# Moving the last layer's patch work and weight rounding from layer 2's attention into layer 1's expert loop

## The chip, the cores and the metric

The kernel runs on one core of a Trainium2 chip. It is one program with one launch. The metric is the device time of one execution in microseconds (us). The time before is 2178.75 us, the median of three runs (2176.64 to 2182.37). Engines are named as in the profile: PE (TensorE matmul), PEld (its weight loads), DVE (VectorE), ACT (ScalarE), POOL (GpSimd), SP (SyncE, which here only issues transfers). A "q" after a name is that engine's queue of instructions.

## The reference

The input x has 32 sequences of 128 tokens with 128 features. Four layers follow, each with an attention-like block over a context of 32 x 128 x 256 and a feed-forward block, both added to x behind a tanh gate:

```python
x = x + tanh(g_xattn[0]) * L0_xattn(ctx, layernorm(x), ...)   # 16 heads, masked by length
x = x + tanh(g_ffn[0])   * L0_ffn(layernorm(x), ...)          # gated MLP, hidden 512
x = x + tanh(g_xattn[1]) * L1_xattn(layernorm(x), ctx, ...)   # 16 heads over context and self
x = x + tanh(g_ffn[1])   * L1_ffn(layernorm(x), ...)          # causal attention, then 8 experts, top 2
x = x + tanh(g_xattn[2]) * L2_xattn(ctx, layernorm(x), ...)   # 8 heads, masked
x = x + tanh(g_ffn[2])   * L2_ffn(layernorm(x), ...)          # 8 experts, top 2
x = x + tanh(g_xattn[3]) * L3_xattn(layernorm(x), ctx, lens)  # patches, below
x = x + tanh(g_ffn[3])   * L3_ffn(layernorm(x), ...)          # ternary weights, 8-bit activations
```

What matters here are two parts of layer 3 that depend on no earlier layer. The first is the patch side of its attention-like block. It reads only the context and the patch lengths:

```python
h_patch = rmsnorm(ctx, g_init)[..., :128]
bidx = cumsum(lens, axis=1) - 1                   # where patches end
boundary = zeros.at[arange(B)[:, None], bidx].set(1)
s = scan(s[t] = a * s[t-1] + u[t])                # a decaying sum over 128 patches
plug = clip(cumsum(boundary, axis=1) - 1, 0, 127)
depool = s[arange(B)[:, None], plug]              # added to layernorm(x)'s projection later
```

The second is the rounding of three 512 x 128 weight matrices to -1, 0 and 1 by the mean of their absolute values.

## The kernel before

The 32 sequences are handled in 8 groups of NB = 4; x stays in SBUF for the whole kernel. The stages, in order, are:

- layer 0 and layer 1 (attention, MLP, causal attention), until about 1260 us of the profiled execution;
- layer 1's experts (`routes1.run`, called at L1214);
- layer 2's attention, from about 1420 us (`attend` at L1371), with the routing of its tokens to experts;
- layer 2's experts (`routes2.run`, L1391) from about 1782 us;
- layer 3, from about 1980 us, which reads `depool`, `wq` and `winv`.

**Layer 1's experts.** Tokens lie in DRAM in blocks of 512, sorted by expert. `Routes.run` is a generator that handles 23 such tiles: 8 with a fixed expert, 15 whose expert is read from a table that is made on the way (`tables`). For each tile, `load` issues the expert's weights `w` (three buffers) and the tokens `xt` on SP's queue. `first` turns the tokens (four PE transposes, `tpe` L838), copies them to `xT` on ACT (L1196), and makes the hidden values: PE `p` (L1203, L1205), ACT `sil` (L1207), DVE `hid` (L1208). `second` multiplies by the second weight (PE `ye` L851) and evicts on ACT (`yT` L1212); `third` turns the result back (four PE transposes), copies it on DVE (`yt` L858) and stores it through SP (L859). The generator yields once after the first two loads, once after the table, and once for each tile, 25 times in all. The caller's loop does nothing with these yields:

```python
for _ in routes1.run(pool, psum, e1_d, E1, turned, swiglu, 2, finish):
    pass
```

In the same stretch POOL clears the eight buffers that layer 2's attention will use for its stacked queries and keys (`Slots`, two memsets each, L355 and L357). These are written in the program ahead of the experts.

**Layer 2's attention.** A `Pipe` runs the attention in turns. Each group has two units of four heads, and each unit two turns. A turn computes scores `sc` (PE L561) and their maxima `mx` (DVE L592), then for an earlier turn the transposed scores `sct` (PE), weights `w` (ACT L627) and products `av` (PE L644). Beside the turns go `before(g)` (adds the experts' results, normalises, makes queries), `after(g)` (adds the attention output, normalises, routes the tokens), the indirect transfers of tokens on POOL (`got` L886, `by_expert_r` L699), and a list called `fill`: generators that are advanced by one piece, that is to their next `yield`, twice a turn (`beside`).

**The last layer's generator.** `last_layer()` (L1236) is the only entry in layer 2's `fill` (L1323). Its pieces are:

1. once: the lengths are cast (`lens` L1240), summed by a matmul (`pe` L1242), and made into end positions (L1244 to L1247);
2. for each of the 8 groups, six pieces: (a) a 0/1 matrix of the ends (`hot` L1253) and two loads from the context on SP (`ck` L1257, `cv` L1259); (b) four small matmuls (`cnt` L1263), their minimum (`bound` L1266), and the root mean square of `ck` and `cv` (`rms_scale`: eight `bst` L218, `bmv`, `ms` and the addition of epsilon L207 on DVE, then the power `r` L208 on POOL); (c) the scaling of `ck` (four, L1271); (d) the decaying sum as one matmul (`pd` L1276), evicted on ACT (`dep` L1278); (e) the running count of ends (`pg`, four, L1284) and the one-hot matrix that selects patches (`pick` L1289, L1290); (f) the bias (L183) and the selection (`pdp`, four, L1295), evicted on ACT (L1299) and stored by SP (`depool` L1300);
3. once: the sums of the three weight matrices (`sums` L1306, `pm` L1310, `wsc`, `winv`);
4. three times: one weight matrix is rounded (`wt` L1318, L1319, `wq` L1320).

That is 1 + 8 x 6 + 1 + 3 = 53 pieces. `ck`, `cv`, `hot`, `dep` and `pick` have one buffer each, so a group's load waits until the group before it has finished with the buffer.

A matmul in float takes two passes, so one matmul in the source is two MATMUL records.

**What sets the order.** The framework puts the instructions of each engine into one in-order queue. The queue is not simply the order of the text: an instruction that waits for data may be passed by a later one that does not. Earlier text goes first where both could run. The sums of the weights (L1306), written last, run at 1420.05 us, before anything else of the generator but the lengths.

Of the kernel before, what the change touches and what calls it, by code (L numbers as in the profile page):

```python
# [12 lines left out]
F32 = mybir.dt.float32  # L13
F32R = mybir.dt.float32r
BF = mybir.dt.bfloat16
I32 = mybir.dt.int32
AF = mybir.ActivationFunctionType
ALU = mybir.AluOpType
AX = mybir.AxisListType
PSUM = bass.MemoryType.PSUM  # L20
DRAM = bass.MemoryType.DRAM

P = 128
# [49 lines left out]
def tile_flamingo_gated(  # L73
# [149 lines left out]
    def bc(a, n=D):  # L223
        return a[:, :, None].to_broadcast([a.shape[0], a.shape[1], n])

    def rms_scale(pool, *parts):

        mv = moments(pool, *parts)
        ms = pool.tile([P, NB], F32, tag="st", name="ms")
        nc.vector.tensor_tensor(ms, mv[:, :, 0], mv[:, :, 0], ALU.mult)  # L230
        nc.vector.tensor_tensor(ms, ms, mv[:, :, 1], ALU.add)
        return rsqrt(pool, ms)
# [52 lines left out]
    def flat(a):  # L285
        return a.rearrange("p b s -> p (b s)")
# [900 lines left out]

    with ExitStack() as outer:
        slots2 = outer.enter_context(tc.tile_pool(name="slots2", bufs=1))
        queries = Slots(slots2, "q2", 4, 8, (64, 96), (nc.gpsimd,))  # L1190
        keys = Slots(slots2, "k2", 4, 8, engines=(nc.gpsimd,))
        with ExitStack() as stack:
            pool, psum = mlp_pools(stack, "f1")

            def turned(xT, tp):
                nc.scalar.mul(xT, tp, COL(col, "g2"))  # L1196

            def swiglu(w, xT):
                hid = pool.tile([P, 2, 512], F32, tag="hid", name="hid", bufs=3)
                for f in range(2):  # L1200
                    fs = slice(f * P, (f + 1) * P)
                    p1 = psum.tile([P, 512], F32, tag="h", name="p1", bufs=3)
                    nc.tensor.matmul(p1, lhsT=E1(w, "w1")[:, fs], rhs=xT, start=True, stop=True)  # L1203
                    p3 = psum.tile([P, 512], F32, tag="h", name="p3", bufs=3)
                    nc.tensor.matmul(p3, lhsT=E1(w, "w3")[:, fs], rhs=xT, start=True, stop=True)  # L1205
                    sil = pool.tile([P, 512], F32, tag="sil", name="sil", bufs=3)
                    nc.scalar.activation(sil, p1, AF.Silu)  # L1207
                    nc.vector.tensor_tensor(hid[:, f, :], p3, sil, ALU.mult)  # L1208
                return hid

            def finish(yT, w, y):
                nc.scalar.copy(yT, y)  # L1212

            for _ in routes1.run(pool, psum, e1_d, E1, turned, swiglu, 2, finish):  # L1214
                pass


        with ExitStack() as stack:
# [14 lines left out]
            stacks = Stacks(8, 16, queries, [keys], "bias2")  # L1233
            at2, gots = {}, {}

            def last_layer():  # L1236


                lens = pool.tile([P, B], F32, tag="lens", name="lens", bufs=1)
                nc.vector.tensor_copy(lens, lens_i)  # L1240
                pe = psum.tile([P, B], F32, tag="tp", name="pe")
                nc.tensor.matmul(pe, lhsT=CST(cst, "tri"), rhs=lens, start=True, stop=True)  # L1242
                ends = pool.tile([P, B], F32, tag="ends", name="ends", bufs=1)
                nc.vector.tensor_scalar(ends, pe, -1.0, None, ALU.add)  # L1244
                wrap = pool.tile([P, B], F32, tag="wrap", name="wrap", bufs=1)
                nc.vector.tensor_scalar(wrap, ends, 0.0, float(P), ALU.is_lt, ALU.mult)
                nc.vector.tensor_tensor(ends, ends, wrap, ALU.add)  # L1247
                bound = pool.tile([P, B], BF, tag="bound", name="bound", bufs=1)
                yield
                for g in range(NG):  # L1250
                    bs = slice(g * NB, (g + 1) * NB)
                    hot = pool.tile([P, NB, P], BF, tag="hot", name="hot", bufs=1)
                    nc.vector.tensor_tensor(  # L1253
                        hot, CST(cst, "iota_s")[:, None, :].to_broadcast([P, NB, P]), bc(ends[:, bs], P), ALU.is_equal,
                    )
                    ck = pool.tile([P, NB, D], F32, tag="ck", name="ck", bufs=1)
                    nc.sync.dma_start(out=ck, in_=ctx_all[bs, :, 0:D].rearrange("b s d -> s b d"))  # L1257
                    cv = pool.tile([P, NB, D], F32, tag="cv", name="cv", bufs=1)
                    nc.sync.dma_start(out=cv, in_=ctx_all[bs, :, D:].rearrange("b s d -> s b d"))  # L1259
                    yield  # L1260
                    cnt = psum.tile([P, NB], F32, tag="tp", name="cnt")
                    for b in range(NB):
                        nc.tensor.matmul(  # L1263
                            cnt[:, b : b + 1], lhsT=hot[:, b, :], rhs=ones_b[:, 0:1], start=True, stop=True
                        )
                    nc.vector.tensor_scalar(bound[:, bs], cnt, 1.0, None, ALU.min)  # L1266

                    r = rms_scale(pool, ck, cv)
                    yield
                    for b in range(NB):  # L1270
                        nc.vector.scalar_tensor_tensor(  # L1271
                            ck[:, b, :], ck[:, b, :], r[:, b : b + 1], ROW(row, "g_init"), ALU.mult, ALU.mult
                        )
                    yield
                    pd = psum.tile([P, NB, D], F32, tag="tp", name="pd")
                    nc.tensor.matmul(flat(pd), lhsT=CST(cst, "decay"), rhs=flat(ck), start=True, stop=True)  # L1276
                    dep = pool.tile([P, NB, D], F32, tag="dep", name="dep", bufs=1)
                    nc.scalar.copy(dep, pd)  # L1278
                    yield

                    pg = psum.tile([P, NB, P], F32, tag="tp", name="pg")
                    for b in range(NB):
                        at = g * NB + b
                        nc.tensor.matmul(  # L1284
                            pg[:, b, :], lhsT=bound[:, at : at + 1].to_broadcast([P, P]), rhs=CBF(cbf, "tri"),
                            start=True, stop=True,
                        )
                    pick = pool.tile([P, NB, P], F32, tag="pick", name="pick", bufs=1)
                    nc.vector.tensor_scalar(flat(pick), flat(pg), -1.0, 0.0, ALU.add, ALU.max)  # L1289
                    nc.vector.tensor_scalar(flat(pick), flat(pick), float(P - 1), iota_p, ALU.min, ALU.is_equal)  # L1290
                    yield
                    po = psum.tile([P, NB, D], F32, tag="tp", name="pdp")
                    with_bias(po, "b_in")
                    for b in range(NB):
                        nc.tensor.matmul(  # L1295
                            po[:, b, :], lhsT=pick[:, b, :], rhs=dep[:, b, :], start=False, stop=b == NB - 1,
                            skip_group_check=True,
                        )
                    nc.scalar.copy(dep, po)  # L1299
                    nc.sync.dma_start(out=depool[g], in_=flat(dep))  # L1300
                    yield

                names = ("gate", "up", "down")
                sums = pool.tile([P, 3], F32, tag="sums", name="sums", bufs=1)
                for i, n in enumerate(names):
                    nc.vector.tensor_reduce(  # L1306
                        sums[:, i : i + 1], W3(w3, n), AX.X, ALU.add, apply_absolute_value=True
                    )
                pm = psum.tile([P, 3], F32, tag="tp", name="pm")
                nc.tensor.matmul(pm, lhsT=ones, rhs=sums, start=True, stop=True)  # L1310
                wsc = pool.tile([P, 3], F32, tag="wsc", name="wsc", bufs=1)
                nc.vector.tensor_scalar(wsc, pm, 1.0 / (D * 512), 1e-5, ALU.mult, ALU.max)
                nc.vector.reciprocal(wsc, wsc)
                nc.vector.reciprocal(winv, wsc)
                yield
                for i, n in enumerate(names):
                    t = pool.tile([P, 512], F32, tag="pick", name="wt", bufs=1)
                    nc.vector.tensor_scalar(t, W3(w3, n), wsc[:, i : i + 1], MAGIC, ALU.mult, ALU.add)  # L1318
                    nc.vector.tensor_scalar(t, t, -MAGIC, -1.0, ALU.add, ALU.max)  # L1319
                    nc.vector.tensor_scalar(wq[n], t, 1.0, None, ALU.min)  # L1320
                    yield

            pipe.fill.append(last_layer())  # L1323

            def before(g):
                if g == 0:
# [302 lines left out]
```

## Time and profile before

| | |
|---|---|
| three runs, median (lowest to highest) | 2178.75 us (2176.64 to 2182.37) |
| the profiled execution's own time | 2170.34 us |
| its span | 2168.5 us |
| mean granted PE clock | 0.86 |
| PE busy | 1658.0 us, 76% of the span |
| DVE busy | 1197.4 us, 55% |
| ACT busy | 894.0 us, 41% |
| POOL busy | 638.6 us, 29% |
| sixteen memsets on POOL | 1261.27 to 1317.40 us |
| first pieces of the generator | 1419.9 us (lengths), 1440.2 us (first matmul) |
| last piece | ends at about 1688.4 us |

The profile has one execution. Its page gives each engine's busy time, the span in 40 slices, the chain of waits that ended last, and the costliest groups of instructions. The trace behind it answers narrower questions: busy times and the granted clock in chosen stretches (the table by stage), the instructions in order of time, one line's or one tile's instructions, and who waited for whom. Times are counted from the start of the span. A line with "x4" merges four instructions; the number ahead of the engine is the time from the first one's start to the last one's end. What stands in brackets with an arrow is the idle time before the line and what ended it. Matmuls overlap, so a single one's duration is longer than its step to the next.

### The profile page before, as it was taken

How to read it: one execution, taken by the hardware profiler on the slowest of the kernel's cores; microseconds unless marked ns; L12 is line 12 of the kernel's file. 1: busy time of each engine (PE TensorE's matmuls, PEld its weight loads, DVE VectorE, ACT ScalarE, POOL GpSimd, SP SyncE). 2: the span in 40 equal slices, each digit the busy share in tenths (PEclk: the TensorE clock that was granted, in tenths of full speed). 3: DMA queues.
4: the chain of work that ended last, by engine and by line, in shares of the span. 5: the costliest groups of instructions: out<-in, count | busy, mean ns of one | idle time of the engine just before them, and what ended most of it. 6: DMA issues, size and time to landing. Idle time of an engine off the chain costs nothing.

```text
span 2168.5 us, 35498 instructions
## 1 busy us (share of the span) xinstructions
PE 1658.0 (76%) x13624; PEld 1010.3 (47%) x13624; DVE 1197.4 (55%) x3504; ACT 894.0 (41%) x1110; POOL 638.6 (29%) x637
## 2 busy tenths in 40 slices
PE   0599998989999999878777569926666629995355
PEld 0455445456656666555455424414555514442223
DVE  7645446475545476766666433357667631113797
ACT  0376565565787745333323223301111204441244
POOL 5101101020000012454544482056443430003550
PEclk9999999999999999987877779966667759997566
DMA  6564558634332343112212035435344212332110
GB/s 214 154 230 154 187 184 266 219 101 124 105 100 67 94 145 84 51 54 59 56 48 55 25 116 174 141 104 148 110 124 121 71 63 101 135 132 86 41 49 20
DMA packets 164536, 244.66 MB, mean 113 GB/s; under 512 B 20560, under 2 KB 102288, under 8 KB 164112
## 3 DMA queue, kind: packets, MB, share of 16 engines
q1 hardware_dynamic: 156176, 225.62, 34.0%
q0 software_dynamic: 8192, 16.79, 2.7%
q8 instruction: 107, 1.75, 0.4%
q14 instruction: 61, 0.50, 0.1%
HBM read 139.74 MB, written 101.24 MB: 111 GB/s over the span
## 4 chain that ended last, share of the span: by engine, by line
PE 40%; DVE 14%; POOL 13%; issue 8%; ACT 2%; DMA 2%; SPq 0%; POOLq 0%; DVEq 0%; ACTq 0%
PE ye L851 5%; PE ph L1382 4%; PE av L644 4%; POOL by_expert_r L699 4%; PE sct L561 4%; POOL got L886 3%; PE sc L561 3%; PE ph L1037 3%; PE p L1203 2%; PE tpe L838 2%; DVE mx L592 2%; PE p L1205 2%; PE tp L282 1%; POOL r L208 1%; POOL w L249 1%
## 5 line engine op out<-in xcount | busy, mean ns | idle before, releaser
L627 ACT ACTIVATE w<-sct 128x1024 f32<-128x1024 f32 x288 | 292.8, 1024 | 346.4 <-PE sct L561 345.2
L592 DVE TENSOR_REDUCE mx<-sc 128x8 f32<-128x1024 f32 x160 | 194.9, 1220 | 130.0 <-PE sc L561 129.6
L561 PEld LDWEIGHTS <-stack_q 96*128 96x128 bf16 x2560 | 194.4, 110 | 134.5 <-issue 104.3
L886 POOL DMA_INDIRECT got<-by_expert_r,slot_r x128 | 127.7, 998 | 360.8 <-issue 335.0
L597 DVE TENSOR_REDUCE mx<-sc 128x4 f32<-128x1024 f32 x128 | 152.9, 1222 | 132.8 <-PE sc L561 132.3
L644 PE MATMUL av<-w,va 128*9 128x128 f32 (+2 forms) x3584 | 198.1, 295 | 36.7 <-POOL w L630 31.9
L561 PE MATMUL sc<-stack_k,stack_q 96*128 96x128 bf16 x1536 | 145.7, 244 | 46.8 <-DMA stack_k<-k 17.4
L561 PE MATMUL sct<-stack_q,stack_k 128*128 128x128 bf16 (+1 forms) x1536 | 139.5, 236 | 17.3 <-DVE mx L592 8.3
L561 PEld LDWEIGHTS <-stack_k 128*128 128x128 bf16 (+1 forms) x1536 | 111.8, 107 | 69.6 <-issue 66.6
L644 PEld LDWEIGHTS av<-w,va 128*9 128x9 f32 (+2 forms) x3584 | 98.6, 94 | 87.5 <-POOL w L630 43.5
L851 PE MATMUL ye<-hid,w 128*128 128x512 f32 x276 | 133.4, 593 | 2.3 <-DVE hid L1208 2.3
L311 POOL CAST hml<-whole 128x512 bf16<-128x512 f32 (+1 forms) x48 | 30.1, 626 | 343.0 <-ACT whole L310 166.7
L1037 PE MATMUL ph<-h,w 128*128 128x512 f32 x256 | 123.7, 610 | 1.8 <-ACT hn L1040 0.9
L1037 PE MATMUL ph<-hn,w 128*128 128x512 f32 x256 | 121.2, 604 | 0.7 <-ACT hn L1040 0.7
L208 POOL TENSOR_TENSOR r<-r,m 128x4 f32<-128x4 f32 x56 | 58.5, 1044 | 188.8 <-DVE r L207 175.0
L561 PE MATMUL sc<-stack_l,stack_q 96*128 96x128 bf16 x1024 | 110.4, 238 | 0.0
L650 ACT COPY ot<-av 128x512 f32<-128x512 f32 x112 | 65.5, 584 | 99.5 <-PE av L644 96.6
L630 POOL TENSOR_SCALAR_AFFINE_SELECT w<-w 128x1024 f32<-128x1024 f32 x64 | 70.8, 1106 | 113.9 <-ACT w L627 113.7
L561 PE MATMUL sct<-stack_q,stack_l 128*128 128x128 bf16 x1024 | 98.9, 234 | 2.7 <-DVE mx L592 2.7
L627 ACT ACT_TABLE_LOAD x72 | 92.4, 1283 | 9.7 <-PE sct L561 8.5
L699 POOL DMA_INDIRECT by_expert_r<-yn,slot_r x64 | 65.6, 1025 | 83.1 <-DVE slot_r L757 25.4
L656 PE MATMUL tpo<-cst,ot 128*128 128x128 f32 x448 | 82.4, 306 | 9.5 <-ACT ot L650 6.9
(295 smaller groups left out, 3290.5 us busy)
## 6 DMA issues: line engine op xcount, KB each, us to landing
by_expert_r<-zeros SPq DMA_DIRECT2D x40, 1024.0 KB
stack_q<-q SPq DMA_DIRECT2D x96, 288.0 KB
stack_k<-k SPq DMA_DIRECT2D x96, 288.0 KB
k<-hml SPq DMA_DIRECT2D x16, 1152.0 KB
w<-in_e_dram SPq DMA_DIRECT2D x23, 514.5 KB
xt<-by_expert_r SPq DMA_DIRECT2D x46, 256.0 KB
by_expert_r<-yt SPq DMA_DIRECT2D x46, 256.0 KB
q<-hml SPq DMA_DIRECT2D x72, 128.0 KB
```

Source lines behind the costliest of these rows:

```text
L208: nc.gpsimd.tensor_tensor(r, r, m05.to_broadcast([P, NB]), ALU.pow)
L561: nc.tensor.matmul(dst[:, h * P : (h + 1) * P], lhsT=stat[rows, 4 * e + h, b], rhs=mov[rows, 4 * e + h, b], start=start and h == e == 0, s ...
L592: latest["maxima"] = nc.vector.tensor_reduce(mx[:, :, b0 : b0 + 2].rearrange("p h b -> p b h"), sc.rearrange("p i (h k) -> p i h k", h=4), ...
L597: nc.vector.tensor_reduce(mx[:, :, b0], sc.rearrange("p i (h k) -> p h i k", h=4), AX.XY, ALU.max, negate=True,)
L627: latest["weights"] = nc.scalar.activation(w.rearrange("p i h k -> p i (h k)"), sc, AF.Exp)
L644: nc.tensor.matmul(av[32 * h : 32 * h + dv + 1, b * P : (b + 1) * P], lhsT=values[c][:, b, 4 * u + h, :], rhs=w[:, i, h, :], start=c == 0, ...
L656: nc.tensor.transpose(tp[:, b].rearrange("p s r -> p (s r)"), ot[:, b, :], ident)
L699: ins = nc.gpsimd.indirect_dma_start(out=self.rows(), out_offset=bass.IndirectOffsetOnAxis(ap=slots, axis=0), in_=rows, in_offset=None,)
L851: nc.tensor.matmul(y, lhsT=w2[:, f, :], rhs=hid[:, f, :], start=f == 0, stop=f == n_f - 1)
L886: ins = nc.gpsimd.indirect_dma_start(out=got[:, k, b, :], out_offset=None, in_=self.rows(), in_offset=bass.IndirectOffsetOnAxis(ap=self.sl ...
L1037: nc.tensor.matmul(ph, lhsT=wt[:, c, f * P : (f + 1) * P], rhs=h[:, c, :], start=c == 0, stop=c == 3)
L1382: nc.tensor.matmul(ph, lhsT=E2(w, "w1")[:, f * P : (f + 1) * P], rhs=xT, start=True, stop=True)
```

## The change

The generator is moved ahead of layer 1's experts, unchanged but for its pools. Its SBUF tiles come from a pool of their own, `patches`, which lives through layer 1's experts and layer 2. Its PSUM tiles come from `place[0]`: in the expert loop one bank of a new pool, in layer 2 the three shared banks that it used before. The caller of the expert loop now advances the generator twelve times at the first yield and once at each of the others; layer 2's `fill` gets what is left of it.

```diff
     with ExitStack() as outer:
         slots2 = outer.enter_context(tc.tile_pool(name="slots2", bufs=1))
+        patch_pool = outer.enter_context(tc.tile_pool(name="patches", bufs=2))
+        place = [None]
+
+        def last_layer():
+            lens = patch_pool.tile([P, B], F32, tag="lens", name="lens", bufs=1)
+            nc.vector.tensor_copy(lens, lens_i)
+            pe = place[0].tile([P, B], F32, tag="tp", name="pe")
...
+            yield
+            for g in range(NG):
...
+                ck = patch_pool.tile([P, NB, D], F32, tag="ck", name="ck", bufs=1)
+                nc.sync.dma_start(out=ck, in_=ctx_all[bs, :, 0:D].rearrange("b s d -> s b d"))
...
+        patches = last_layer()
         queries = Slots(slots2, "q2", 4, 8, (64, 96), (nc.gpsimd,))
...
-            for _ in routes1.run(pool, psum, e1_d, E1, turned, swiglu, 2, finish):
-                pass
+            place[0] = stack.enter_context(tc.tile_pool(name="patches_ps", bufs=1, space=PSUM))
+            for i, _ in enumerate(routes1.run(pool, psum, e1_d, E1, turned, swiglu, 2, finish)):
+                for _ in range(12 if i == 0 else 1):
+                    next(patches)
...
-            def last_layer():
-                lens = pool.tile([P, B], F32, tag="lens", name="lens", bufs=1)
...
-            pipe.fill.append(last_layer())
+            place[0] = psum
+            pipe.fill.append(patches)
```

## The prediction

> **What bounds the kernel now.** I read the table by stage first, with stretches cut at the borders of layer 1's experts (1265 to 1414 us, 23 tiles) and of layer 2's attention (1440 to 1745), because the change takes work from the second and puts it into the first.
>
> ```profile
> core 0: us, PE busy (x) PEld busy (x) DVE busy (x) ACT busy (x) POOL busy (x), PEclk, DMA share, GB/s
> 1265.00:1288.00 23.00, 20.02 (x57) 9.48 (x57) 11.84 (x20) 8.31 (x13) 22.83 (x7) 0.87 0.29 100
> 1288.00:1351.00 63.00, 62.11 (x199) 29.50 (x199) 19.80 (x30) 23.14 (x40) 29.17 (x9) 1.00 0.58 176
> 1351.00:1414.00 63.00, 63.00 (x200) 29.59 (x198) 19.80 (x30) 24.06 (x41) 0.00 (x0) 1.00 0.43 136
> 1560.00:1620.00 60.00, 35.77 (x340) 27.85 (x338) 40.48 (x168) 9.75 (x14) 34.17 (x35) 0.68 0.44 127
> 1620.00:1690.00 70.00, 47.41 (x478) 39.78 (x478) 49.61 (x215) 14.31 (x20) 27.36 (x28) 0.72 0.40 115
> 1690.00:1745.00 55.00, 37.59 (x456) 31.14 (x455) 32.94 (x138) 13.73 (x18) 18.87 (x18) 0.74 0.21 62
> ```
>
> Columns are start and end, then busy time by engine. PE is the bound of the experts: busy 63.00 of 63 us at clock 1.00, while DVE has 31% and ACT 38%. In layer 2 nothing is: PE is 60 to 68% busy at clock 0.68 to 0.74, DVE 60 to 71%, POOL 34 to 57%; the stage is a chain through in-order queues. So a piece moved into the experts is free on DVE and ACT, and is paid in full on PE.
>
> The order of time at the start of the experts shows a second thing:
>
> ```profile
> 1268.29 6.98 POOL L357 MEMSET stack_q<- 32x4096 bf16 x2
> 1272.08 3.23 DVE L801 CAST table<-row 1x30 int32<-1x30 f32 x1
> 1272.17 3.14 DVE L1208 TENSOR_TENSOR hid<-p,sil 128x512 f32<-128x512 f32 x2
> 1275.33 6.97 POOL L355 MEMSET stack_q<- 128x4096 bf16 x2
> 1275.39 1.13 PE L851 MATMUL ye<-hid,w 128*128 128x512 f32 x2 [2.28 <-DVE hid L1208]
> ...
> 1310.44 6.96 POOL L357 MEMSET stack_k<- 3x4096 bf16 x2
> ```
>
> Sixteen memsets of 3.51 us fill POOL from 1261.27 to 1317.40. A DVE cast of 30 numbers lasts until the memset beside it ends (3.23 us), hid behind it too, and PE idles 2.28 us.
>
> **The change, part by part.** The generator has 53 pieces: 1 for the lengths, 6 for each of 8 groups, 1 for the sums, 3 for the weights. The expert loop yields 25 times (loads, table, 23 tiles), so 12 + 24 = 36 pieces move: the lengths, groups 0 to 4 whole, and five of group 5. The other 17 stay at the head of layer 2's fill.
>
> *PE in the experts.* Prices at clock 1.00 come from steps between matmuls of one line:
>
> ```profile
> 1412.34 1.88 PE L851 MATMUL ye<-hid,w 128*128 128x512 f32 x4
> ...
> 532.39 0.89 PE L1099 MATMUL po<-wa,oT 128*128 128x128 f32 x6
> ...
> 531.22 0.40 PE L561 MATMUL sct<-stack_q,stack_k 128*128 128x128 bf16 x4
> ```
>
> A float pass of 512 columns steps by (1.88 - 0.59)/3 = 0.43, of 128 columns by (0.89 - 0.275)/5 = 0.12 (0.107 to the next line's start), a bf16 one by 0.056. Per group: pd L1276 2 x 0.43 = 0.86; pdp L1295 8 x 0.11 = 0.88; its bias L183, 512 columns of bf16, 0.22; pg L1284 4 x 0.056 = 0.22; cnt L1263 4 x 0.06 = 0.25. That is 2.43 us. Five groups 12.2, group 5 without pdp and bias 1.3, pe L1242 0.1: **+13.6 us**, all on the path, as PE has no free time there. Below: a tile's period is 6.26 us (p L1203 starts at 1288.34, 1294.60, 1300.86) and its own steps add to 12 x 0.43 + 8 x 0.107 = 6.0, so 0.25 a tile is open; with a piece in two gaps of three, some 4 us of the 13.6 would be hidden. I take none, as PE already waits there for xT on ACT, whose queue gets longer.
>
> *Queues in the experts.* DVE gets about 6.4 us a group (hot 0.68, 8 statistics at 0.2, 4 ck at 0.35, pick 0.69 + 0.48, some 1.5 in small ones), beside 43 us of free DVE in every 63; ACT gets 11 dep copies of 0.59, beside 39 free. Cover gone, a dep copy ahead of xT L1196 costs up to 0.59. SP gets 12 context loads (0.4 to 0.57 each) and 5 depool stores (0.35), between weight loads that already wait there for ye (53.2 us in all): a ck load stuck behind one comes up to a tile late, and bst, then hid, wait on DVE. A depool store that waits for its dep copy on ACT holds the weight, token and result transfers behind it on SP; a pd that waits for ck on DVE holds the next tile's p and ye behind it on PE. POOL gets 6 powers r of 1.04, all emitted behind the memsets: group 0's r cannot start before 1317.4, tile 8, so the pieces behind it bunch up and are worked off from there. For these mismatches, some 25 PE pieces at 0 to 0.3 us: between 0 and 8, I take **+3**.
>
> *The start.* Three DVE instructions of the cast's kind come under the memsets: lens L1240, wrap L1246, and the 128x4 addition in group 0's r (L207). The first has nothing behind it but its own chain; each other can hold DVE up to one memset, 3.5 us, before hid of tile 0, which ends PE's wait. Bounds 0 and 7; I take one, **+3.5**. Sum in the experts: **+20**, between 10 and 29.
>
> *Layer 2.* What goes is read twice. The chain of waits holds the pieces often; one group's passage:
>
> ```profile
> 1580.67 1.05 POOL r L208
> 1581.73 0.03 issue
> 1581.75 1.58 DVE ck L1271 x4
> 1583.34 0.04 issue
> 1583.38 2.07 PE pd L1276 x2
> ```
>
> PE stood for r and ck and then ran pd. Adding all chain rows of such pieces from 1503 to 1666 (r, ck, hot, pick, bst, pd, pdp) gives 27 us. That is the upper end: another wait stands behind each. The other reading compares like with like, cutting at the ends of the 16 output copies ot L650, one for half a group:
>
> ```profile
> 1645.20:1664.38 19.18, 11.77 (x118) 10.39 (x117) 11.98 (x43) 2.76 (x5) 8.76 (x9) 0.64 0.56 161
> 1664.38:1682.24 17.86, 12.03 (x120) 9.70 (x119) 13.79 (x60) 3.80 (x5) 4.11 (x5) 0.81 0.29 89
> 1682.24:1700.31 18.07, 14.35 (x117) 11.72 (x117) 11.53 (x50) 2.86 (x4) 6.02 (x5) 0.55 0.36 106
> ```
>
> None of these has a fetch (got L886 ends at 1609). With the half before (17.91), full fill costs 18.55 a half; with about half the fill (pdp of group 7, the weights) 17.97. So a whole fill is worth 2 x 0.58 = 1.2 us a half, and 36 pieces, four a half, are 9 halves: 10.5 us. Prologue work is no part of it: POOL's fetches bind 1420 to 1500, and the 17 remaining pieces lie there as the first 13 do now. I take **-13**, nearer the like-for-like row, since it contains what takes the chain's place.
>
> Of the clock the rows say that it stood at 0.68 where PE was 60% busy, at 0.72 and 0.74 where it was 68%, at 1.00 where it was full. A rule of the Trainium skill speaks against the change here: "TensorE: Matmul & The Clock Gate", Part 1, says that the clock is throttled unless PE's recent activity releases it. By that rule the thinner layer 2 would run its remaining matmuls slower: a fall of 0.03, my estimate, on some 60 us that PE holds of that chain is 2.5 us, and the sum would be +9.5 instead of +7. My sum goes without it.
>
> **Sum.** 13.6 + 3 + 3.5 - 13 = +7 us. The profiled execution took 2170.34 (span 2168.5), 8.4 below the median of 2178.75; on the median it gives **2186**. A measurement can tell about 0.3% of this kernel, 6.5 us, from no change.
>
> **The rivals.**
> 1. *The chain's rows count in full: faster.* Layer 2 gives 27 us and the experts cost only 10 to 17: -10 to -17, about 2165. The place is the PE queue of layer 2, where scores wait behind pd and pdp. It decides from 20 us on, 2.2 us a half. For it: the passage above, 5.5 us in one group. Against: halves with less fill are hardly shorter.
> 2. *The start hurts twice.* Both stalls (7), mismatches of 8, PE 13.6, give 29; with layer 2 at -10, +19 to +22: 2198 to 2201.
> 3. *Group 0's r blocks a queue.* If DVE's or PE's queue has ck or pd of group 0 ahead of a tile's work, it stands until 1317: some 45 us more, about 2225. Against: the queue orders follow lengths of work, not the text; stack_k's loads, written in layer 2, go out at 1294.74 on SP, shortly after that slot's memset, and SP waited for no memset in that stage.
> 4. *Nothing net.* The gaps hide 4 us and the start costs nothing: 13.6 - 13, about 2179.
>
> **How the numbers follow.** Forecast 40% (own range 2181 to 2192; 13 of it within 0.3%, 27 above), rival 1 30% (faster), rival 2 15%, rival 3 5%, rival 4 10% (7 within, 3 faster). Faster 0.33, same 0.20, slower 0.47. The range of 2160 to 2208 goes from rival 1's lower end (2162) with 2 us more to the experts' upper 29 with nothing won back; outside stay rival 3 and the tails of 1 and 2.
>
> **What would show it.** The 23 tiles should end about 20 us later against their start, PE still full, and more so from tile 8 on, where pieces bunch; hid of tile 0 should start later than 1275.3, measured from the first memset. No r of these groups before the sixteenth memset's end. Layer 2 from its first fetch to its last store should be shorter by 13, with pd's 16 passes at 592 ns and not 1061. I am wrong if the halves fall to 16 us or less (rival 1), or if PE idles for tens of us before 1317 (rival 3).

## The result, and the profile after

The changed kernel took 2193.88 us (median of 5 runs, 2190.1 to 2194.67), the kernel before 2178.75 (5 runs, 2176.37 to 2182.37): 1.0065 times the time, 95% interval 1.005 to 1.008. It is slower, by some 15 us (0.65%) where I had 7. The profiled execution of the changed kernel took 2190.1 us (span 2188.1), 3.8 below its median.

This number can't be understood without one thing that the experiments brought out: layer 2's attention runs in two ways, with the same instructions, a *quick* one and a *slow* one. The changed kernel's runs above are slow ones, and the one profile of before that the forecast was read from was quick.

By stage, cut at the first expert's weight load (L827), the first fetch of layer 2 (L886) and the first weight load of layer 2's experts:

| stage, us | before, profile | changed, profile | difference | predicted |
|---|---|---|---|---|
| up to the experts | 1261.0 | 1255.8 | -5.2 | 0 |
| layer 1's experts | 159.8 | 181.1 | +21.3 | +20 |
| layer 2's attention | 360.5 | 364.1 | +3.6 | -13 |
| the rest | 387.1 | 387.1 | 0 | 0 |

Up to the experts every engine has the same instructions in the same order in both, so the -5.2 is not the change's. The experts by stage, changed kernel (start and end, length, busy time of PE, its weight loads, DVE, ACT and POOL with instruction counts, granted clock, DMA share, GB/s):

```profile
1255.81:1278.80 22.99, 14.04 (x35) 6.65 (x36) 17.72 (x45) 4.98 (x7) 22.57 (x7) 0.69 0.47 154
1278.80:1341.80 63.00, 61.35 (x217) 29.74 (x216) 25.88 (x67) 23.35 (x40) 35.31 (x12) 1.00 0.57 179
1341.80:1404.80 63.00, 61.49 (x228) 30.99 (x227) 34.13 (x105) 24.63 (x41) 4.03 (x4) 1.00 0.52 166
```

PE is still the bound: 61.4 of 63 us at clock 1.00, now with 1.6 us of idle time where there was 0.9 and none (62.11 and 63.00 of 63), and with 217 and 228 matmuls where there were 199 and 200. DVE went from 19.8 to 25.9 and 34.1 us and has half its time left. Over the whole stage PE's busy time is 164.2 us against 147.4 (+16.8), its idle time 16.9 against 12.4 (+4.5).

Layer 2, two halves of one group without a fetch, and two rows of what PE waited for from 1500 to 1770 us (columns of the second: engine and line, what ended the wait, us in all, times, longest):

```profile
1677.00:1699.30 22.30, 10.98 (x124) 8.82 (x125) 10.29 (x33) 2.63 (x3) 9.49 (x9) 0.71 0.27 72
1699.30:1710.70 11.40, 10.61 (x95) 8.72 (x94) 7.47 (x37) 2.86 (x4) 0.00 (x0) 0.52 0.43 129
```

```profile
PE sc L561 <- DVE mx L592: 37.7, 6, 7.5
PE sc L561 <- issue: 13.7, 20, 1.1
```

Before, a half took about 18; here it is 22.3 and 11.4, 33.7 a group against 36. The short half is dense (PE busy 10.61 of 11.40) and runs at clock 0.52. The new row is "issue": PE stood, 20 times, although no wait that the trace records held it.

### The profile page after: what moved, and what is told of

The parts are those of the page before. It is cut to its first block, busy times and chain, and to the rows that moved or that the text cites. A ratio compares the mean times of both kernels' runs of the same rounds, so it can differ in the third digit from the quotient of the medians.

```text
span 2188.1 us, 35509 instructions
## 1 busy us (share of the span) xinstructions
PE 1665.9 (76%) x13618; PEld 1014.9 (46%) x13624; DVE 1202.8 (55%) x3504; ACT 895.3 (41%) x1110; POOL 636.1 (29%) x637
## 4 chain that ended last, share of the span: by engine, by line
PE 42%; DVE 13%; POOL 12%; issue 8%; ACT 2%; DMA 2%; another core or an unknown queue 0%; SPq 0%; POOLq 0%; DVEq 0%; ACTq 0%
PE ye L851 5%; PE av L644 4%; POOL by_expert_r L699 4%; PE sct L561 4%; PE ph L1389 4%; PE ph L1037 4%; PE sc L561 4%; POOL got L886 3%; PE tpe L838 2%; PE p L1294 2%; PE p L1296 2%; DVE mx L592 2%; PE tp L282 1%; PE tpo L656 1%; POOL w L249 1%
## 5 line engine op out<-in xcount | busy, mean ns | idle before, releaser
L644 PE MATMUL av<-w,va 128*9 128x128 f32 (+2 forms) x3584 | 203.6, 300 | 34.3 <-POOL w L630 27.3
L886 POOL DMA_INDIRECT got<-by_expert_r,slot_r x128 | 127.9, 999 | 263.9 <-issue 231.6
L561 PE MATMUL sct<-stack_q,stack_k 128*128 128x128 bf16 (+1 forms) x1536 | 147.4, 244 | 22.0 <-DVE mx L592 7.7
L561 PEld LDWEIGHTS <-stack_k 128*128 128x128 bf16 (+1 forms) x1536 | 117.6, 111 | 76.8 <-issue 73.9
L1389 PE MATMUL ph<-xT,w 128*128 128x512 f32 x184 | 87.7, 620 | 0.8 <-DVE nx L779 0.8
```

Source lines behind the costliest of these rows:

```text
L561: nc.tensor.matmul(dst[:, h * P : (h + 1) * P], lhsT=stat[rows, 4 * e + h, b], rhs=mov[rows, 4 * e + h, b], start=start and h == e == 0, s ...
L644: nc.tensor.matmul(av[32 * h : 32 * h + dv + 1, b * P : (b + 1) * P], lhsT=values[c][:, b, 4 * u + h, :], rhs=w[:, i, h, :], start=c == 0, ...
L886: ins = nc.gpsimd.indirect_dma_start(out=got[:, k, b, :], out_offset=None, in_=self.rows(), in_offset=bass.IndirectOffsetOnAxis(ap=self.sl ...
L1389: nc.tensor.matmul(ph, lhsT=E2(w, "w1")[:, f * P : (f + 1) * P], rhs=xT, start=True, stop=True)
```

## The experiments

Theory 1 at the outset: layer 2's attention is a closed chain, the pieces lay in its idle time, and taking them out gives nothing. Theory 2: the gain of 10 to 13 us was there and something new ate it. The two stages of the profiled runs, in us (the two runs of the last section come there); the occasion is the one found below, and each median stands beside that of the kernel before in the same comparison:

| kernel | pieces in experts / layer 2 | occasion | experts | layer 2's attention | median | before |
|---|---|---|---|---|---|---|
| before, two profiles | 0 / 53 | quick | 159.8, 159.6 | 360.5, 360.5 | | |
| changed, no piece moved | 0 / 53 | slow | 161.0 | 374.0 | 2182.13 | 2179.23 |
| twelve moved | 12 / 41 | slow | 168.6 | 372.0 | 2184.07 | 2179.23 |
| changed, first profile | 36 / 17 | slow | 181.1 | 364.1 | 2193.88 | 2178.75 |
| changed, third profile | 36 / 17 | slow | 180.2 | 359.6 | 2188.55 | 2178.82 |
| all moved | 53 / 0 | slow | 188.2 | 363.9 | 2199.98 | 2179.23 |
| 36 left out, twice | 0 / 17 | slow | 162.1, 160.4 | 358.1, 352.9 | 2165.03, 2159.72 | 2179.23, 2178.82 |
| changed, second profile | 36 / 17 | quick | 179.5 | 330.6 | 2157.09 (one run) | 2168.22 |
| 36 moved, late | 36 / 17 | quick | 178.2 | 329.5 | 2157.64 | 2168.22 |
| 35 into the prologue | 0 / 53 | quick | 161.5 | 369.0 | 2176.22 | 2168.22 |

Only the changed kernel was profiled in both ways. The kernel before was never profiled in the slow one; the kernel in which no piece moves stands for it there.

### Nothing moved, pools kept

```diff
             for i, _ in enumerate(routes1.run(pool, psum, e1_d, E1, turned, swiglu, 2, finish)):
-                for _ in range(12 if i == 0 else 1):
+                for _ in range(0):
                     next(patches)
```

> The changed kernel's pools, with no piece moved: all 53 stay in layer 2's fill. Theory 1 (in layer 2 the pieces fill time in which the closed chain of a group keeps PE and DVE idle, so taking them away gains almost nothing): the same as before, within 4 us, the attention stage of layer 2 at about 360 us. Theory 2 (the gain of 10 to 13 us in layer 2 was there, and the new pools and tile places ate it): this kernel carries that cost and no gain, so it is 8 us or more slower than before, the stage at 368 to 374.

1.0015 times before (1.0001 to 1.0029): the new pools cost 0 to 6 us, less than the 8 of theory 2. Yet layer 2's attention took 374.0 in this profile, not 360, which by itself is the top of theory 2's range. Against the first profile of before, the stage is 13.5 us longer and the way up to the experts 6.5 shorter. Since the timed runs differ by 3 us only, I read it as the first sign that 360.5 was not the usual passage of the kernel before.

### The pieces of groups 0 to 5 left out

```diff
-                for _ in range(12 if i == 0 else 1):
+                for _ in range(0):
...
-            for g in range(NG):
+            for g in range(6, NG):
...
-                nc.sync.dma_start(out=flat(dp), in_=depool[g])
+                nc.sync.dma_start(out=flat(dp), in_=depool[max(g, 6)])
```

> Nothing is moved, and the pieces of groups 0 to 5 are left out altogether (the last layer reads the patches of group 6 in their place, so its loads are the same): layer 2 has 17 pieces as in the changed kernel, and the experts have none. This prices 36 pieces in layer 2 alone. Experts as before, 160 us from the first weight load to the first fetch. Theory 1: layer 2's attention 356 to 366 us, the kernel within 5 us of before. Theory 2 in the size that I predicted: 347 us, the kernel 10 to 13 us faster than before. By the rows of the chain of waits in full: 334 us, 27 us faster.

0.9935 times before (0.9918 to 0.9951), 14.2 us less; repeated below, 0.9917 (0.9902 to 0.9932), 19.1 less. So 36 pieces (here six whole groups) do cost time in layer 2, and 14 to 19 us of it, somewhat more than the 13 that I had predicted. Theory 1 falls: its 356 to 366 us hold the stage's 358.1, but it had the kernel within 5 us of before.

### Twelve moved, and all 53

```diff
-                for _ in range(12 if i == 0 else 1):
+                for _ in range(12 if i == 0 else 0):
```

> Only the twelve pieces at the first yield are moved (the lengths, group 0, five pieces of group 1); none goes beside a tile, 41 stay in layer 2. Both theories for the experts: PE 2.43 + 1.33 + 0.1 = 3.9 us and the start about 3, so 165 to 168 us instead of 160. Theory 1 for layer 2: 358 to 362, the kernel 5 to 8 us slower than before. Theory 2: 3 us less in layer 2, the kernel 2 to 4 us slower.

```diff
-                for _ in range(12 if i == 0 else 1):
-                    next(patches)
+                for _ in range(12 if i == 0 else 2):
+                    next(patches, None)
```

> All 53 pieces go into the experts (twelve at the first yield, two at each one after), none is left in layer 2. Experts: PE 8 x 2.43 + 0.1 = 19.5 us, the start 3, mismatches 3 to 6: 186 to 189 us instead of 160. Theory 1: layer 2's attention 355 to 365, the kernel 20 to 30 us slower than before. Theory 2: 15 us less in layer 2 (345), the kernel 10 to 14 us slower. By the rows of the chain: 40 us less, the kernel 12 us faster.

1.0023 (1.0012 to 1.0033) and 1.0092 (1.0075 to 1.0109). Against 160.5 us, the mean of the seven profiles with no piece emitted there (one of the last section included), the experts grew by 8.1, by 19.7 (mean of four: three of the changed kernel and one of the last section) and by 27.7. Between 12 and 53 pieces that is 19.6 us for 15.6 us of PE by the prediction's prices (3.9 and 19.5), 1.26 a microsecond, and 3.2 us are left at zero. The first expert result gives nearly as much: ye comes 17.0 us after the first weight load where pieces are moved (12, 36 or 53), 14.4 where none is. By the second tile ye is 4.0 to 4.4 us late in all of them. In the changed kernel the rows are these (start, us, what, in brackets the idle time before it and what ended it):

```profile
1263.12 6.99 POOL L357 MEMSET stack_q<- 32x4096 bf16 x2
...
1266.68 3.44 DVE L799 TENSOR_SCALAR row<-row 1x15 f32<-1x15 f32 x1
...
1270.28 0.85 DVE L218 BATCH_NORM_STATS2 bst<-ck 128x6 f32<-128x128 f32 x4
1271.06 0.84 DVE L218 BATCH_NORM_STATS2 bst<-cv 128x6 f32<-128x128 f32 x4
...
1272.16 0.62 DVE L1299 TENSOR_TENSOR hid<-p,sil 128x512 f32<-128x512 f32 x1
...
1272.84 1.69 PE L851 MATMUL ye<-hid,w 128*128 128x512 f32 x2 [4.13 <-DVE hid L1299]
```

A table step of 15 numbers lasted until the memset beside it ended (3.44 us, to 1270.12 beside 1270.11; the step before it, L797, took 2.90). In the kernel before, two steps met memsets as well (L799 and the cast L801), and hid ended with the second, 14.3 us after the first weight load. Here the second ended at 14.3 too, and eight statistics of group 0 then went ahead of hid.

Layer 2 shows something that neither theory has: with 17 pieces it takes 358.1 where they were left out, 364.1 where they were moved, and with none at all 363.9.

### Two more profiles

Both kernels unchanged, for a second execution with a profile.

> The kernel before, unchanged, for a second profiled execution: the first one (2170.3 us) lay 8 us below the median of its runs. If that is the passage through layer 2's attention, this one has a stage of about 369 us there instead of 360.5 and takes 2177 to 2182; if the 8 us came from elsewhere, the stage is 360 again and another stage is longer.

> The changed kernel, unchanged, for a second profiled execution. Experts 181 us again (both theories). Layer 2's attention: 364 to 368 us. If its first output copy comes 81 us after the first fetch again and not 73, the longer prologue belongs to the kernel and not to one execution.

This comparison had the kernel before at 2168.22 us (18 runs, 2162.26 to 2175.1) and the changed kernel at 2157.09: faster, by 11. The second profile of before matches the first within 0.2 us in the experts, layer 2 and the rest, 360.5 in layer 2 again. The changed kernel's second profile has the experts at 179.5 and layer 2 at 330.6, 33 less than in its first, with the same instructions in the same order on every engine. Changed kernel, quick, the same two halves as above and four stretches cut at the changes of the granted clock:

```profile
1659.90:1676.20 16.30, 10.41 (x108) 8.84 (x109) 10.12 (x33) 2.63 (x3) 5.78 (x6) 0.58 0.38 106
1676.20:1685.10 8.90, 7.24 (x111) 6.02 (x111) 7.43 (x38) 2.86 (x4) 3.70 (x4) 1.00 0.66 195
...
1660.54:1674.20 13.66, 8.41 (x72) 7.52 (x76) 8.42 (x26) 1.02 (x1) 4.39 (x4) 0.50 0.40 111
1674.20:1691.26 17.06, 11.78 (x185) 9.65 (x186) 11.96 (x56) 5.49 (x7) 6.75 (x7) 1.00 0.61 166
1691.26:1701.50 10.24, 6.12 (x61) 4.95 (x64) 6.44 (x17) 1.02 (x1) 4.67 (x5) 0.50 0.08 27
1701.50:1718.57 17.07, 13.09 (x222) 10.89 (x211) 11.16 (x53) 7.07 (x9) 8.46 (x10) 1.00 0.12 38
```

The first profile, slow, cut in the same way:

```profile
1682.86:1693.10 10.24, 5.83 (x57) 4.70 (x60) 6.00 (x15) 1.02 (x1) 4.64 (x6) 0.50 0.08 26
1693.10:1696.52 3.42, 2.00 (x31) 1.18 (x30) 0.22 (x1) 0.00 (x0) 2.50 (x4) 1.00 0.12 40
1696.52:1710.17 13.65, 10.85 (x92) 9.18 (x92) 7.88 (x35) 2.86 (x4) 0.95 (x1) 0.50 0.38 109
1710.17:1716.99 6.82, 2.91 (x43) 2.48 (x43) 3.80 (x19) 1.61 (x2) 1.66 (x1) 1.00 0.59 161
```

The clock changes in steps of 3.41 us (3.42, 6.82, 10.24, 13.65). On the quick occasion it rises after 10 to 14 us and stays at 1.00 for 17, over the whole dense half: 8.9 us. On the slow one it rises, falls after 3.42, and the dense half goes at 0.50: 11.4 us. The slow pattern repeats every 34.1 us, ten of those steps; the next one began at 1716.99.

Of the 8.5 us by which the slow group is longer (33.7 against 25.2), the dense half at the lower clock is 2.5. The other 6.0 lie in the long half, 22.3 against 16.3, and there the clock was higher on the slow occasion (0.71 against 0.58) and PE's busy time nearly the same (10.98 and 10.41). So most of the difference is PE standing, not PE running slower.

What stands around the clock's fall is in the order of time. Slow:

```profile
1691.76 0.30 PE L611 MATMUL tpn<-cbf,negp 128*48 128x128 bf16 x1
1691.99 1.12 PE L282 MATMUL tp<-cst,yn 128*128 128x128 f32 x4
1693.03 0.64 PE L644 MATMUL av<-w,va 128*17 128x128 f32 x16
...
1693.72 0.45 PE L561 MATMUL sc<-stack_k,stack_q 96*128 96x128 bf16 x5
1694.68 0.38 PE L561 MATMUL sc<-stack_k,stack_q 96*128 96x128 bf16 x4 [0.51 <-issue]
1695.41 0.22 PE L561 MATMUL sc<-stack_k,stack_q 96*128 96x128 bf16 x1 [0.34 <-issue]
1696.14 0.33 PE L561 MATMUL sc<-stack_k,stack_q 96*128 96x128 bf16 x3 [0.52 <-issue]
1697.58 0.48 PE L561 MATMUL sc<-stack_k,stack_q 96*128 96x128 bf16 x3 [1.11 <-issue]
...
1696.13 0.22 DVE L613 COPY mrows<-tpn 48x128 bf16<-48x128 bf16 x1 [4.84 <-remote]
1697.61 0.81 DVE L1365 TENSOR_SCALAR fT<-tp,col 128x512 f32<-128x512 f32 x1 [1.27 <-remote]
...
1699.32 0.59 ACT L650 COPY ot<-av 128x512 f32<-128x512 f32 x1 [7.41 <-PE sc L561]
```

Quick, the same instructions:

```profile
1674.70 0.24 PE L611 MATMUL tpn<-cbf,negp 128*48 128x128 bf16 x1
1674.86 0.66 PE L282 MATMUL tp<-cst,yn 128*128 128x128 f32 x4
1675.45 0.63 PE L644 MATMUL av<-w,va 128*17 128x128 f32 x16
...
1676.13 1.07 PE L561 MATMUL sc<-stack_k,stack_q 96*128 96x128 bf16 x16
...
1674.97 0.22 DVE L613 COPY mrows<-tpn 48x128 bf16<-48x128 bf16 x1 [0.34 <-PE tpn L611]
1675.56 0.81 DVE L1365 TENSOR_SCALAR fT<-tp,col 128x512 f32<-128x512 f32 x1 [0.37 <-PE tp L282]
...
1676.20 0.58 ACT L650 COPY ot<-av 128x512 f32<-128x512 f32 x1 [0.94 <-PE av L644]
```

On the slow occasion 16 scores took 4.3 us instead of 1.1, and what waits for PE came late too: mrows 4.1 us after tpn's end (quick: 0.03), ot 5.6 us after av's (quick: 0.1). PE is thin for 5 us, and the clock falls. The same measure tells all profiles apart: the copy fT (L1365) of groups 4 and 5, counted from 0, came 2.3 to 5.1 us after the last of its transposes in the nine profiles that the table and the last section call slow, 0.0 us in the five called quick (in group 1 of the changed kernel it is late in both ways, 3.4 us in the slow profile and 4.2 in the quick one). It lies under POOL's row stores L699, one every 1.27 us and each 0.97 us long, which the quick passage has too, in the same order and as long. What sets an occasion I don't know; whether it goes by occasion alone isn't shown either, since 18 of the 19 runs of before beside the first four experiments took 2174.9 us or more and one 2170.7.

### The 36 pieces late

```diff
-                for _ in range(12 if i == 0 else 1):
-                    next(patches)
+                for _ in range(0 if i < 10 else 12 if i == 10 else 2 if i < 21 else 1):
+                    next(patches, None)
```

> The same 36 pieces go beside the experts, but none before the tenth yield's tile, by which the memsets are over: twelve there, then two or one a tile. If the price of 21 us in the experts is PE's own time (13.6) and waits beside the tiles (1.2 to 1.3 us for each us of PE, as 12 and 53 pieces cost 8 and 27), the experts take 177 to 179 us instead of 181 and hid of tile 0 starts as in the kernel before; the kernel is 2 to 4 us faster than the changed one. If the start and the memsets made most of it, the experts take 172 or less and the kernel is as fast as before. If bunching is what costs, it is no faster than the changed one.

0.9953 times before (0.9935 to 0.9972): faster, by 10.6 us, on the quick occasion, beside 2157.09 for the changed kernel in one run there. The experts took 178.2 against 179.5. The start was not won back: ye came 18.0 us after the first weight load, as three table steps waited for a memset (2.90, 3.44 and 3.32 us, hid behind the last) where two did before (3.44 and 3.23).

The edit moved less than it says. In the engines' queues the first pieces stood further ahead than in the text: lens, the weight sums and hot of groups 0 and 1 still ran in the first 6 us after the first weight load, as in the changed kernel, and the first pd came 75.6 us after it, where the changed kernel had 67.7 (its quick profile); the pd of groups 1 to 4 came 8 to 26 us later than there. So the total of 178.2 lies in the predicted 177 to 179, but not for the predicted reason. By the steps of ye from tile to tile, the pieces cost 13.4 us behind the second tile, where the changed kernel's three profiles have 15.5 to 16.9: that is PE's price of 13.6 with next to nothing for waits, and the start, 5.0 us by the second tile, took back some of what this gave. A version without any piece's instruction under the memsets was not run. (In the kernels with no piece in the experts, lens, the sums and group 0's r ran there too.)

### 35 pieces into layer 2's prologue

```diff
+            def beside(g):
+                for _ in before(g):
+                    if g == 0:
+                        for _ in range(7):
+                            pipe.advance(pipe.fill)
+                    yield
+
-            layer = Layer(stacks, before, lambda g: at2[g], after, ahead=2)
+            layer = Layer(stacks, beside, lambda g: at2[g], after, ahead=2)
```

> None of the pieces goes beside the experts. Seven pieces are emitted behind each of the five steps with which layer 2 prepares group 0, 35 in all, so that they fall into the 75 us from the first fetch to the first output copy, in which PE is busy a third of the time and DVE a half; 18 stay in the fill. If what they cost in layer 2 (14 us by the kernel that leaves them out) is the company of the scores, it goes: experts 161, the stage 358 to 362 plus some 5 us for five powers on POOL among the fetches, the kernel 5 to 10 us faster than before. If the prologue is as tight as the rest (each piece on DVE ahead of a fetch's addition), it is longer by up to 6.4 us of DVE a group, 32 us, and the kernel is 10 to 20 us slower than before.

1.0035 (1.0021 to 1.0049): slower by 8, outside both ranges, nearer the second. The first output copy came 110.2 us after the first fetch (73.5 before), 36.7 later; from it to the last the stage took 221.0 instead of 249.4. The prologue, in the second profile of before and here:

```profile
1420.10:1493.60 73.50, 24.67 (x220) 18.92 (x221) 43.20 (x155) 6.92 (x10) 48.75 (x55) 0.57 0.43 122
```

```profile
1422.60:1532.80 110.20, 55.44 (x333) 37.48 (x330) 67.79 (x270) 14.30 (x22) 57.23 (x65) 0.56 0.38 113
```

DVE got 24.6 us more and PE, at clock 0.56, 30.8 more: a prologue with half its DVE idle had no room. In its place the stage behind it became 28.4 us shorter, so the 35 pieces cost 36.7 us here and had cost 28.4 there.

### The changed kernel again, and the left-out pieces again

> The changed kernel, unchanged, timed against the kernel before once more. In its first profile PE issued in bursts with 31 gaps (over 0.3 us, that no wait explains) in layer 2's attention, 47 us with the waits behind them; in its second one, 2157.1 us, there was no such gap, and neither in the two profiles of the kernel before. If the gaps belong to an occasion and not to the kernel, then without them the experts are 20 us longer and layer 2's attention 30 us shorter (330 instead of 360), and the kernel is 9 to 12 us faster than before; with them, 364 us and 12 to 16 us slower. Anything between speaks against this reading.

> Again nothing moved and the pieces of groups 0 to 5 left out. On an occasion with the gaps it was 14 us faster than before, layer 2's attention 358 us. Without them, by the theory that layer 2 is a chain in which each piece's rows count (27 us), the stage is 330 to 333 us and the kernel 27 to 31 us faster than before; by the price of halves that I compared (10 to 13 us), it is 347 to 350 and 10 to 13 us faster.

1.0039 (1.0025 to 1.0053), 9.7 us slower, and 0.9917 (0.9902 to 0.9932). Both profiles are slow by the measure of fT, but neither met the numbers expected with the gaps: 359.6 us and 9.7 slower lie between the two cases (364, 12 to 16 slower), which by the words above speaks against the reading as it stood, with two fixed ways; 352.9 and 19.1 lie between as well. The slow way has a spread of its own, some 5 us. Within the slow way, layer 2 took 364.1 and 359.6 in the changed kernel, 358.1 and 352.9 without the pieces anywhere. The 6 us between them are lost between the fourth and the eighth output copy, while fetches still run; why, I did not separate. The quick way of the left-out kernel was not seen.

### PE kept busy in the wait

Six passes per group that nobody reads, behind the last half of each group:

```diff
+                if n_warm[0] and u == n_units - 1:
+                    idle = psum.tile([P, 512], F32, tag="tp", name="idle")
+                    for _ in range(n_warm[0]):
+                        nc.tensor.matmul(idle, lhsT=ident, rhs=flat(o), start=True, stop=True)
...
             stacks = Stacks(8, 16, queries, [keys], "bias2")
+            n_warm[0] = 6
```

> The changed kernel, and behind the last half of each group of layer 2 six extra float passes of 512 columns whose result nobody reads (o times the identity, into a tile of their own): they fall into the 7 us in which PE waits for the group's DVE chain and last 5.2 us at full clock. In the slow occasion a group took 33.6 us, and the granted clock went 1.00 for 3.4 and 6.8 us and 0.50 for 13.7 and 10.2, a period of 34.13 us; in the quick one 25 to 27 us. Theory clock (the gate falls to 0.5 in that wait, so the next dense half runs at half speed and the group locks to the gate's rhythm): the halves behind the wait go at 1.00, a group takes 27 us or less from group 4 on, and layer 2's attention is 335 to 345 us also on a slow occasion, 20 to 30 less than the changed kernel there. Theory chain (DVE's and POOL's steps set the period whatever the clock): 360 to 364 as before on a slow occasion, 330 on a quick one, or up to 20 more where the extra passes hold a score.

> The same six passes a group in the kernel before, with all 53 pieces in layer 2's fill. Theory clock: on a slow occasion layer 2's attention 350 to 360 us, the kernel 10 to 20 us faster than the kernel before; the gain is smaller than in the changed kernel, since its fill keeps PE busy for part of the wait already. Theory chain: no gain, up to 20 us slower.

Both on a slow occasion (before 2180.98). In the changed kernel nothing came of it: 1.0037 (1.0021 to 1.0053), layer 2 at 362.0. In the kernel before, 0.9902 (0.9867 to 0.9937), 2160.15 us, 20.8 less: on such an occasion this beats both kernels. Its layer 2 took 355.6, against 374.0 with the same 53 pieces and no passes, in the kernel with nothing moved on an earlier slow occasion. The changed kernel with the passes:

```profile
1679.05 7.68 PE L668 MATMUL idle<-o,cst 128*128 128x512 f32 x12 [0.81 <-DVE o L661]
1686.57 1.06 PE L563 MATMUL sc<-stack_k,stack_q 96*128 96x128 bf16 x16
...
1693.66 0.18 PE L183 MATMUL pl<-three,cbf 3*128 3x32 bf16 x1
1698.69 1.66 PE L1379 MATMUL pl<-wg,fT 128*128 128x8 f32 x7 [4.84 <-DVE fT L1372]
```

```profile
1701.30:1714.60 13.30, 10.88 (x103) 9.24 (x103) 8.09 (x39) 2.74 (x4) 0.00 (x0) 0.51 0.27 76
```

The kernel before with them, the long half of the seventh group and the short one behind it:

```profile
1684.30:1706.00 21.70, 15.81 (x139) 9.29 (x138) 11.79 (x45) 2.65 (x4) 9.41 (x9) 0.92 0.27 80
1706.00:1716.30 10.30, 10.30 (x114) 9.16 (x114) 7.08 (x37) 3.85 (x6) 0.00 (x0) 0.67 0.01 2
```

In the first, the passes filled one wait and the clock fell in the next (4.84 us for fT, late as above), so the dense half went at 0.51 again. In the second the long half went at 0.92, where the nothing-moved kernel had 0.69 for the same half (0.67 for that of the group before). Yet it took 21.7 us against 22.1 there, and in the changed kernel the stage's mean clock rose from 0.63 to 0.69 without any gain. So the passes are worth 20.8 us in the kernel before, but that the clock is what they save is not shown: they also move everything behind them, and 13 of the 18 us in the stage are won by the end of the sixth group's first half, against the nothing-moved kernel. That the clock makes the slow way is not shown either, as fT was late here too. This version's quick way was not seen.

## Why the prediction was right or wrong

**The experts: right in sum, roughly in parts.** +20 predicted, +19.7 over four profiles. PE's 13.6 us, all on the path, came out a little low: its busy time grew by 16.8 (15.0 with the pieces late). The start's 3.5: ye of the first tile was 2.6 late (17.0 against 14.4), of the second 4.0 to 4.4. PE's 13.6 and the mismatches' 3 together: 15.5 to 16.9 behind the second tile. The memsets were foreseen at the start, but through lens, wrap and r; what cost there was eight statistics of group 0 that went ahead of hid when the second held table step had ended.

**Layer 2's attention: the term of -13 failed, against the profile it was set on.** It came out at +3.6, then -0.9. In the slow way the size of the work was about right: 36 pieces left out are worth 14.2 and 19.1 us, and the changed kernel lies 10 and 14 below the nothing-moved one (374.0). What failed is the base: 360.5 us was a quick passage, while the timed runs that the forecast was put on (2178.75) were slow. The 8.4 us between profile and median were taken as a constant to be added; in the nothing-moved kernel, the slow one nearest to before, this very stage is 13.5 us longer and the way up to the experts 6.5 shorter. For the quick way the choice between the two readings was wrong: 330.6 against 360.5 is -30, near the chain's 27 and far from the halves' 10.5. I had compared halves with full fill (18.55) to halves with half of it (17.97) and doubled the step, 1.2 us a half. The quick halves with no fill took 16.3 and 8.9, 12.6 on the mean: 6 us less, not 1.2. (The passage quoted for rival 1 is 4.8 us from its first row to its last, not 5.5.)

**The rivals.** Rival 1 (chain rows in full, 2165) is what the quick occasion shows in layer 2: 10.6 and 11 us faster than before, by -30 there and +18 to +20 in the experts, where it had allowed 10 to 17. The sign that I had set for it, halves of 16 us or less, came there too (12.6 on the mean), and only there: the slow halves, 22.3 and 11.4, are 16.9 on the mean. Rival 2 (start twice) did not happen. Rival 3 fell: the first r came after the memsets and PE, idle for 16.9 us in the whole stage, never stood tens of us for it. Rival 4 fell: even the late pieces cost 13.4 us for a price of 13.6, so nothing was hidden in the tiles' gaps.

**The sum.** 2186 against 2193.88 and, on another slow occasion, 2188.55. The slow sum is +20 in the experts, about -12 in layer 2 against the nothing-moved kernel, and the 3 us that this kernel itself lost: +11, beside +15.1 and +9.7 measured. That 2193.88 lies in the range of 2160 to 2208 is owed to its width, which took in rivals 1 and 2; the forecast's own range, 2181 to 2192, missed it, and that the kernel came out slower at all was the luck of the occasion: on the quick one it was faster.

**What would show it.** As told: the experts 20 longer with PE nearly full, most of it from tile 8 on, no r before the last memset, the second pass of pd at 592 or 593 ns against 1061 in the six groups that moved. Not as told: layer 2 by 13; and the two groups that stayed had pd at 1061 in the slow profile.

**The clock.** The Trainium skill, "TensorE: Matmul & The Clock Gate", Part 1, says that the gate works in windows of 3413 ns and that one idle window brings half speed. The trace agrees in the step (3.42, 6.82, 10.24, 13.65 us) and in the two values, 0.50 and 1.00; the step behind which the clock fell at 1696.52 was not idle, though, as PE was busy for 2.00 of its 3.42 us. The fall of 0.03 that I had set aside was too much for the mean of the stage: on the quick occasion 0.66 before and 0.64 in the changed kernel, on the slow occasion 0.65 (nothing moved) and 0.63. What I had not seen is that it matters where the half speed lies: one dense half is 11.4 us at 0.52 and 8.9 at 1.00.

## What to carry to other kernels

Where the profiled execution lies off the median by more than the effect you look for, find the stage in which it does before you add the terms: here the 8 us had to do with a second way of running the stage under change. A piece of work has a price in every stage (36 pieces: 20 us in the experts, 14 to 19 or 30 in layer 2; 35 pieces: 37 in the prologue); leave the piece out to measure the price where it stands before moving it. In a loop with a serial wait longer than a few microseconds, look at the granted clock of the dense part behind the wait: here it was worth 2.5 us a group. And look in the trace where moved work really ran: its place in the queues isn't its place in the text.

## What the runs showed of the hardware that I had not expected

- The same program has two passages through one stage: 330.6 and 364.1 us in the changed kernel, with the same instruction order. On slow occasions PE's results reached DVE and ACT 2 to 6 us late and its own scores stood (16 in 4.3 us instead of 1.1), beside POOL's row stores; the stores lasted as long in both (0.97 us). That the stores are the cause was not tried, and it is open.
- The clock changed in steps of 3.41 us, and on the slow occasion the loop's period was ten of them, 34.1 us, for several groups in a row.
- Matmuls that nobody reads made the kernel before 20.8 us faster (0.9902, 0.9867 to 0.9937), and the changed kernel no faster; why, is open.
